# A two-layer graph network on one core: reordering the second probe in the first two blocks of a step, and one activation table for logarithm and exponential

## The chip, the cores and the metric

One core of a Trainium2 chip. The metric is the device time of one execution in microseconds (us), lower is better; "time" is the median of several executions.

## The reference, cut to what matters

Layer 0 is a graph attention layer over 4096 nodes. Layer 1 runs two steps; each makes a 4096 x 4096 attention matrix, keeps of each row the largest probabilities that sum to 0.9, and multiplies the node features by it. This choice of a row's smallest kept value is what the change is about.

```python
def _top_p_attention(X, W1, W2, W3):
    logits = (X @ W1.T @ W2.T) @ (X @ W3.T).T / TAU
    probs = jax.nn.softmax(logits, axis=-1)
    idx = jnp.argsort(-probs, axis=-1)
    sp = jnp.take_along_axis(probs, idx, axis=-1)
    keep_sorted = jnp.cumsum(sp, axis=-1) - sp < TOP_P       # TOP_P = 0.9
    ...                                                      # mask = keep_sorted, back in place
    A = probs * mask
    return A / jnp.maximum(A.sum(-1, keepdims=True), 1e-12)

for n in range(STEPS):                                       # STEPS = 2
    A = _top_p_attention(Xa, W1, W2, W3)
    Xf = R @ Xf
    Xa = A @ Xa
    Z = Z + Xf @ U1[n].T + Xa @ U2[n].T
```

## The kernel before

A step works on 32 blocks of 128 rows. ScalarE (ACT) makes a block's exponentials `e`. Three probes, each a sum over all values below a threshold, close in on the row's cut; the second and third run on VectorE (DVE), and GpSimd (POOL) turns each sum of 128 x 1 values into the next threshold, in some 17 tiny instructions. The third probe leaves the values below its threshold in `big`; DVE takes the largest of these (in step 0, 16 instructions that each give the 8 largest of a stretch, called maxima here, then a sort of the best 48), finds the exact cut and masks `e`. TensorE (PE) turns the masked block and multiplies it.

The tables of a step, one row each for nm (the shift of the exponent) and others, come from a logarithm and an exponential:

```python
nc.vector.tensor_copy(sg, var)
nc.scalar.activation(roots, roots, AF.Ln)                # each of the two needed a table load before it
nc.scalar.activation(roots, roots, AF.Exp, scale=0.5)
nc.vector.scalar_tensor_tensor(nm, sg, 4.0, mu, ALU.mult, ALU.add)
```

The probes and POOL's thresholds (`pool` is GpSimd):

```python
def lowered(c, y, more):
    t = col("lowered", 6)
    pool.tensor_tensor(t, inv_e, y, ALU.pow)                       # "the power" below
    pool.tensor_scalar(t, t, c, more, ALU.mult, ALU.mult)
    return t

def first_step(r):                                                 # after ACT's first probe; cut
    ...
    r.y1 = fall(r, L)
    if not last:
        r.c2 = lowered(r.c1, r.y1, 1.0)                            # threshold of the second probe
        pool.tensor_tensor(r.yy, r.y1, r.y1, ALU.mult)
    pool.tensor_tensor(r.up, r.z, mone, ALU.pow)
    ...

def second_probe(r):
    if r.n + 1 == STEPS:
        return                                                     # the last step has none
    L = col("L")
    nc.vector.scalar_tensor_tensor(junk, r.e, r.c2, r.e, ALU.is_le, ALU.mult, accum_out=L)
    y2 = fall(r, L)
    ...                                                            # 11 more instructions on POOL
    r.c3 = lowered(r.c2, y, up)                                    # threshold of the third probe

def third_probe(r):
    r.L = col("L3")
    nc.vector.scalar_tensor_tensor(big, r.e, r.c3, r.e, ALU.is_le, ALU.mult, accum_out=r.L)

def masked(r):
    kept, r.scale = col("kept"), col("scale")
    nc.vector.scalar_tensor_tensor(r.e, r.e, r.t, r.e, ALU.is_ge, ALU.mult, accum_out=kept)
    nc.vector.reciprocal(r.scale, kept)
```

The order of a block (`candidates` is maxima and sort; `finish` and `finish_rows` are small row work of earlier blocks):

```python
def chosen_kept(b):
    r = blocks[b]
    if 0 < b < NB - 1:
        second_probe(blocks[b + 1])
    candidates(r, found)
    if b == 0:
        masked(r)
    if b > 2:
        finish_scale(blocks[b - 3])
    if b + 2 < NB:
        first_step(blocks[b + 2])
    if b == 0:
        second_probe(blocks[1])
    if b + 1 < NB:
        third_probe(blocks[b + 1])
    if b == 0 and last:
        direct_probe(blocks[3])
    if b > 1:
        finish(blocks[b - 2])
    if b > 2:
        finish_rows(blocks.pop(b - 3))
    if b > 0:
        masked(r)
```

## Time and profile before

| | kernel before |
|---|---|
| time, median of 4 executions | 3262.1 us (3259.44 to 3265.22) |
| the execution that the profile was taken in | 3278.6 us |
| step 0 in the profile | 911.6 us |
| step 1 in the profile | 863.1 us |

"Step 0" is counted from the copy into `roots` ahead of its logarithm to the same copy of step 1, "step 1" from there to the end of the span. First the page's busy times:

```profile
span 3276.4 us, 51761 instructions
PE 2973.4 (91%) x19213; PEld 2417.6 (74%) x19213; DVE 2656.6 (81%) x5020; ACT 1952.7 (60%) x2903; POOL 1266.9 (39%) x1793
```

PE is busiest over the whole span, but the share mixes stages; inside step 0 DVE's chain is the bound, as the prediction shows. Then DVE's groups for the third probe (L694) and the second probe (L673). Columns: busy time and mean ns of one; then the idle time just before them, and what ended it.

```profile
L694 DVE SCALAR_TENSOR_TENSOR big<-e,lowered 128x4096 f32<-128x4096 f32 x64 | 286.8, 4482 | 20.9 <-POOL lowered L639 20.9
L673 DVE SCALAR_TENSOR_TENSOR junk<-e,lowered 128x4096 uint8<-128x4096 f32 x32 | 143.5, 4485 | 14.9 <-POOL lowered L639 14.9
```

The 20.9 hold the 7.27 us that the change aims at. The 14.9 before the second probe are 3.3 for block 0 (a fill of the pipeline) and 11.6 in small pieces.

### The profile page before, as it was taken

The numbers are of one execution on the slowest core, as the hardware profiler recorded it, in microseconds if no ns is written. First come the engines' busy times: TensorE is split into PE (matmuls) and PEld (weight loads), VectorE is DVE, ScalarE is ACT, GpSimd is POOL, SyncE is SP. The second block draws the span as 40 slices with busy tenths as digits, with TensorE's granted clock in tenths as the row PEclk, the third lists the DMA queues.
The fourth block names the chain that finished last, engine by engine and source line by source line (L and its number), as shares of the span: only waits on it lengthen the run. The fifth ranks groups of instructions, "written<-read, shape, count | busy, mean of one in ns | idle before, by whom it ended". The sixth has DMA issues, their size and how long they took to land. (4 is left out here: it accounts for less than half of the span.)

```text
span 3276.4 us, 51761 instructions
## 1 busy us (share of the span) xinstructions
PE 2973.4 (91%) x19213; PEld 2417.6 (74%) x19213; DVE 2656.6 (81%) x5020; ACT 1952.7 (60%) x2903; POOL 1266.9 (39%) x1793
## 2 busy tenths in 40 slices
PE   4499899898989999986899999999879999999996
PEld 2299799797977888874677777777757777777785
DVE  6598899998976555546999999999469988888894
ACT  5588687786862110016577776775266777776742
POOL 3200100201000000003798998899015656656530
PEclk8699999999999999997899999999889999999998
DMA  9825639356225555520000000000100000000000
GB/s 260 228 83 144 204 113 255 117 142 206 73 85 181 165 177 164 161 89 1 10 19 15 16 20 15 15 18 17 62 13 10 25 20 25 22 22 25 20 27 13
DMA packets 198314, 268.48 MB, mean 82 GB/s; under 512 B 13728, under 2 KB 155552, under 8 KB 198048
## 3 DMA queue, kind: packets, MB, share of 16 engines
q1 hardware_dynamic: 152272, 207.99, 19.4%
q0 software_dynamic: 16896, 33.56, 5.7%
q10 hardware_dynamic: 28880, 23.48, 2.3%
q8 instruction: 155, 2.54, 0.3%
q14 instruction: 111, 0.91, 0.1%
HBM read 226.77 MB, written 71.76 MB: 91 GB/s over the span
## 5 line engine op out<-in xcount | busy, mean ns | idle before, releaser
L799 PE MATMUL acc<-X,eT 128*128 128x256 f32 x4160 | 978.4, 381 | 0.8 <-ACT eT L793 0.8
L799 PEld LDWEIGHTS acc<-X,eT 128*128 128x128 f32 x4160 | 762.6, 191 | 90.1 <-ACT eT L793 1.9
L291 PE MATMUL acc<-ut,m 128*128 128x195 bf16 (+1 forms) x8192 | 732.2, 249 | 82.3 <-DVE m L279 49.7
L291 PEld LDWEIGHTS <-m 128*128 128x128 bf16 x8192 | 703.4, 98 | 111.1 <-DVE m L279 66.9
L272 ACT ACTIVATE g<-sr,d_big 128x1024 bf16<-128x1024 f32 x512 | 550.6, 1178 | 50.2 <-DVE m L278 40.6
L618 ACT ACTIVATE void<-e,c 128x2048 int8<-128x2048 f32 x244 | 490.4, 2010 | 0.6
L611 ACT ACTIVATE e<-mm,nm 128x1024 f32<-128x1024 f32 x256 | 285.9, 1117 | 341.2 <-PE mm L488 338.1
L432 PE MATMUL racc<-hl,ar 128*128 128x512 f32 x2048 | 469.4, 391 | 16.8 <-issue 10.0
L432 PEld LDWEIGHTS racc<-hl,ar 128*128 128x128 f32 x2048 | 384.5, 188 | 101.5 <-issue 10.8
L791 PEld LDWEIGHTS tp<-ident,e 128*128 128x128 f32 x2080 | 246.8, 143 | 224.2 <-issue 126.6
L793 ACT COPY eT<-tp 128x512 f32<-128x512 f32 x520 | 303.4, 584 | 168.9 <-PE tp L791 168.1
L791 PE MATMUL tp<-ident,e 128*128 128x128 f32 x2080 | 327.9, 281 | 57.0 <-DVE e L728 42.8
L278 DVE TENSOR_TENSOR m<-g,ax 128x2048 bf16<-128x2048 bf16 x256 | 311.7, 1218 | 41.8 <-ACT g L272 38.8
L707 DVE MAX8 cand<-big 128x8 f32<-128x228 f32 (+1 forms) x1088 | 343.9, 395 | 0.1
L279 DVE TENSOR_TENSOR m<-ax,m 128x2048 bf16<-128x2048 bf16 x256 | 317.1, 1239 | 26.9 <-DVE m L278 1.4
L488 PE MATMUL mm<-kT,qT 64*128 64x512 f32 x1024 | 304.8, 678 | 33.5 <-ACT e L611 33.5
L428 DVE CAST ar<-at 128x1024 fp32r<-128x1024 bf16 x256 | 177.0, 692 | 169.8 <-PE racc L432 167.3
L694 DVE SCALAR_TENSOR_TENSOR big<-e,lowered 128x4096 f32<-128x4096 f32 x64 | 286.8, 4482 | 20.9 <-POOL lowered L639 20.9
L728 DVE SCALAR_TENSOR_TENSOR e<-e,found 128x4096 f32<-128x4096 f32 x64 | 286.7, 4480 | 0.0
L443 ACT ACTIVATE xf<-xf,rinv 128x256 f32<-128x256 f32 x64 | 32.7, 510 | 373.3 <-DVE xf L442 373.3
L648 POOL TENSOR_TENSOR sums<-sums 128x4 f32<-128x4 f32 (+1 forms) x64 | 106.4, 1662 | 378.8 <-ACT void L618 231.1
L488 PEld LDWEIGHTS mm<-kT,qT 64*128 64x128 f32 x1024 | 84.3, 196 | 130.6 <-issue 66.7
(245 smaller groups left out, 3269.4 us busy)
## 6 DMA issues: line engine op xcount, KB each, us to landing
at<-adj_d SPq DMA_DIRECT2D x256, 256.0 KB, 3.0
ut<-uv_d SPq DMA_DIRECT2D x60, 784.0 KB, 4.3
ax<-in_adj_t_dram POOLq DMA_DIRECT2D x32, 1024.0 KB, 13.6
adj_d<-ax SPq DMA_DIRECT2D x32, 1024.0 KB, 11.5
uv_d<-parts ACTq DMA_DIRECT2D x32, 392.0 KB, 8.2
xf<-xf_d SPq DMA_DIRECT2D x65, 128.0 KB, 2.0
sr<-s_d SPq DMA_DIRECT2D x16, 512.0 KB, 4.7
xf_d<-xf ACTq DMA_DIRECT2D x64, 128.0 KB, 2.4
```

Of the source, the lines that this page charges most:

```text
L272: nc.scalar.activation(g[:, c, :], shared[k].sr, AF.Relu, scale=BIG, bias=d_big[:, h, j:j + 1])
L278: nc.vector.tensor_tensor(m[0], g, a, ALU.min)
L279: nc.vector.tensor_tensor(m[1], a, m[0], ALU.subtract)
L291: nc.tensor.matmul(shared[k].acc[i][:, t, :cols], m[t][:, c, ts(i, P)], shared[k].ut[j // QUARTER][:, j % QUARTER, t, :cols], start=(j == ...
L432: nc.tensor.matmul(acc[i].rearrange("p s d -> p (s d)"), ar[:, c, ts(i, P)], hl[hop][:, j].rearrange("p s d -> p (s d)"), start=(j == 0), ...
L488: nc.tensor.matmul(pm[:, h, :], q[ts(h, DA), :], kT[ts(h, DA), ts(c, 512)], start=True, stop=True)
L618: nc.scalar.activation(void, r.e[:, ts(h, N // 2)], (AF.Relu, AF.Sign)[i], bias=r.c1, scale=-1.0, accum_out=r.sums[:, h, 2 + i:3 + i])
L694: nc.vector.scalar_tensor_tensor(big, r.e, r.c3, r.e, ALU.is_le, ALU.mult, accum_out=r.L)
L707: nc.vector.max(cand[:, s, :], big[:, edges[s]:edges[s + 1]])
L791: nc.tensor.transpose(pt[:, i, :], r.e[:, ts(4 * g + i, P)], ident)
L793: nc.scalar.copy(eT, pt)
L799: nc.tensor.matmul(r.acc[:, 0, :], eT[:, i, :], cur[:, j, :], start=(j == 0), stop=(j == NB - 1))
```

## The change

The intent of the reordering: in blocks 0 and 1 DVE should not stand idle while POOL makes the next block's third threshold. So the next block's second probe moves in between this block's maxima and their sort, the sort hides POOL's work, and the mask goes ahead of the next third probe, so that PE gets its block sooner. The intent of the other part: a table that holds both functions, loaded once at the start.

```diff
+    nc.scalar.preload_act_table_set("natural_log_exp_and_others")
...
-    def candidates(r, found):
+    def candidates(r, found, between=None):
...
             nc.vector.max(cand[:, s, :], big[:, edges[s]:edges[s + 1]])
+        if between:
+            between()
         nc.vector.tensor_scalar(cum[:, :1], r.z, 1.0 - TOP_P, r.L, ALU.mult, ALU.subtract)
...
                 r = blocks[b]
-                if 0 < b < NB - 1:
+                early = b < (1 if last else 2)
+                if not early and b < NB - 1:
                     second_probe(blocks[b + 1])
-                candidates(r, found)
-                if b == 0:
+
+                candidates(r, found, (lambda: second_probe(blocks[b + 1])) if early else None)
+                if early:
                     masked(r)
                 if b > 2:
                     finish_scale(blocks[b - 3])
                 if b + 2 < NB:
                     first_step(blocks[b + 2])
-                if b == 0:
-                    second_probe(blocks[1])
                 if b + 1 < NB:
                     third_probe(blocks[b + 1])
...
-                if b > 0:
+                if not early:
                     masked(r)
```

Line numbers in the changed kernel are 3 to 5 higher: third probe L697 (before L694), second probe L676 (L673), mask L733 (L728), POOL's power and threshold L641 and L642 (L638 and L639).

## The prediction

> **What bounds the kernel now.** I read the page first, then each engine's timeline where the changed lines run, then DVE's groups with the idle time before them. The last two of four stages are touched: layer 1 runs two steps, step 0 from about 1453 to 2361 us of the span, step 1 to the end. Each step makes its tables (logarithm, then exponentials), fills the first blocks, and then for each of 32 blocks DVE probes, picks candidates and masks, while PE turns and multiplies the masked block. The start of step 0 on DVE:
>
> ```profile
> 1535.75 5.33 DVE L707 MAX8 cand<-big 128x8 f32<-128x256 f32 x16
> ...
> 1546.36 4.48 DVE L728 SCALAR_TENSOR_TENSOR e<-e,found 128x4096 f32<-128x4096 f32 x1
> ...
> 1550.96 4.49 DVE L673 SCALAR_TENSOR_TENSOR junk<-e,lowered 128x4096 uint8<-128x4096 f32 x1
> ...
> 1562.73 4.49 DVE L694 SCALAR_TENSOR_TENSOR big<-e,lowered 128x4096 f32<-128x4096 f32 x1 [7.27 <-POOL lowered L639]
> ```
>
> These are block 0's maxima (L707), its mask (L728), block 1's second probe (L673) and block 1's third probe (L694). The last waits 7.27 us for POOL, which turns the second probe's sum into the third threshold. Later blocks do not have this wait: there the second probe comes before the maxima, and 10.7 us of maxima and sort hide POOL's 7.1 us. PE's side:
>
> ```profile
> 1550.90 1.12 PE L791 MATMUL tp<-ident,e 128*128 128x128 f32 x4 [5.13 <-DVE e L728]
> ...
> 1591.22 1.09 PE L791 MATMUL tp<-ident,e 128*128 128x128 f32 x4 [13.10 <-DVE e L728]
> ...
> 1813.50 0.63 PE L791 MATMUL tp<-ident,e 128*128 128x128 f32 x4 [0.53 <-DVE e L728]
> ```
>
> PE waits 13.10 us for block 1's mask. From block 2 on it needs 24.32 us a block (one block's first transpose at 1642.48, the next at 1666.80) and DVE needs 24.41, or 25.05 where it waits 0.61 for POOL. DVE's masks of blocks 2 and 30 start at 1610.95 and 2306.92, so 24.86 a block. From 1813 us on, PE waits about 0.5 us in most blocks: **DVE's chain sets the end of step 0**. Step 1 has no second probe (the function returns at once), so PE bounds it after its start.
>
> The table loads, step 0 and then step 1, on ACT:
>
> ```profile
> 1500.63 1.28 ACT L554 ACT_TABLE_LOAD   x1
> 1501.93 0.26 ACT L554 ACTIVATE roots<-roots 128x64 f32<-128x64 f32 x1
> 1502.20 1.28 ACT L555 ACT_TABLE_LOAD   x1
> 1503.50 0.26 ACT L555 ACTIVATE roots<-roots 128x64 f32<-128x64 f32 x1
> ...
> 2413.58 1.28 ACT L554 ACT_TABLE_LOAD   x1 [1.35 <-DVE thr L570]
> 2414.87 0.26 ACT L554 ACTIVATE roots<-roots 128x64 f32<-128x64 f32 x1
> 2415.14 1.28 ACT L555 ACT_TABLE_LOAD   x1
> 2416.44 0.26 ACT L555 ACTIVATE roots<-roots 128x64 f32<-128x64 f32 x1
> ```
>
> One load goes before each logarithm and one before the exponential after it. All work of the step waits for this pair, as DVE's nm needs roots.
>
> The last thing I looked at is the end of step 1. The rare repair ran there, for one block:
>
> ```profile
> 3238.62 4.49 DVE L773 SCALAR_TENSOR_TENSOR e<-junk,a_t,e 128x4096 f32<-128x4096 uint8 x1
> ```
> ```profile
> 3243.26 1.08 PE L791 MATMUL tp<-ident,e 128*128 128x128 f32 x4 [11.85 <-DVE e L773]
> ```
>
> A row whose smallest kept and largest dropped value are equal makes its block be done again. Step 0 had none.
>
> **What the Trainium skill says.** "ScalarE: Activation LUTs", section "What ACT_TABLE_LOAD costs", gives about 1283 ns a load and about 1380 ns of drain. The trace agrees on the load (1283 ns mean); between the end of one small activation and the start of the next it shows 1.31 us (2415.13 to 2416.44), so I use the trace's 1.3. The same page, section "Table sets: the hidden batching unit", says that natural_log_exp_and_others holds both functions and that cheap ones (Relu, Copy) are in every set; so no load should remain in the steps. In its terms, "max 1536 buckets" are shared by a set's functions and each fit has its own error budget, so a logarithm from another set may differ in its last bits. No run shows it yet. "SBUF — State Buffer", section "SBUF: two separate sides", says that a DVE operation with two SBUF inputs and a GpSimd operation exclude one another for a whole instruction. The trace agrees: L649 takes about 0.3 us alone and 4.34 beside the DVE probe at 1510.91.
>
> **The change, part one: tables.** The one load at the start moves from 15.02 us to earlier; ACT then idled until 21.47 us for POOL, so nothing is won. In step 0 the first load lay beside DVE's variance (roots ready at 1501.89), so only the second is won: the exponential can follow the logarithm at about 1502.1 in place of 1503.50, 1.4 us. In step 1 the first load started after its wait, at 2413.58, so both are on the path: 2 x 1.3 = 2.6 us. All that follows in a step waits for it. Sum **-4.0 us**.
>
> **Part two: order in step 0.** Step 1 is unchanged by it: its block 0 already had its mask first, and a second probe does nothing. In step 0 no DVE instruction is added or removed. I laid out the new order by hand with the durations above (a 4096-wide probe 4.41 us to the next start, 16 maxima 5.24, sort 5.37), at old times, without the 1.4:
>
> - Block 0's maxima end 1540.99; second probe of 1 to 1545.40; sort to 1550.77; mask 0 to 1555.2 (before 1550.8, so PE starts **4.4 us later**, 1555.3).
> - POOL's 7.1 us for block 1 start at 1545.58; 5.2 us of them fit beside the sort, then the mask locks POOL out until 1555.2, and 1.7 us are left: third probe of 1 at 1556.9, after a wait of **1.5** and not 7.27.
> - POOL's first step of block 2, which used to run at 1540.5, now stands behind this. Its second instruction is locked out by the third probe until 1561.5; the threshold is ready at 1565.1, in time.
> - Block 1: maxima to 1566.65, second probe of 2 to 1571.1, sort to 1576.4, mask 1 to 1580.8 (before 1591.0, **10 us earlier**), third probe of 2 at 1582.5, again after about 1.5.
> - Block 2 goes back to the old order: second probe of 3 first. Its threshold comes from POOL's first step of block 3, which can begin only at 1582.5, is locked out until 1587.2 and needs 3.6 more: 1590.8. DVE is ready at 1587.0 and **waits about 3.8 us**. So this probe starts at about 1590.9; before it started at 1591.19.
>
> DVE's old 7.27 us thus come back as 1.5 + 1.5 + 3.8 = 6.8. PE multiplies block 0 to about 1582, block 1 at once after it to about 1607, and waits for block 2's mask at about 1615, where it used to be at 1618. The 2.7 us it wins are slack ahead of DVE, which bounds the step from block 10 on anyway. Part two: **-0.3 us**, give or take 2, since 19 or so of the blocks have the 0.61 wait and which do is a matter of tens of ns. With part one: 3261.6 - 4.3 = **3257 us**, if the repair stays as it is.
>
> **The rivals.**
> 1. *The new logarithm reshuffles the ties.* nm comes from logarithm and exponential and is added to every logit before rounding. I recomputed both steps in 32-bit arithmetic from the inputs, over 24 rounding orders and with nm moved by about 1e-6 of its size. Step 0's blocks with a tie did not change by the move. Step 1's were drawn anew: of 48 draws 19 had no such block, 17 one, 9 two, 3 more. What each makes of the time, from this trace: without a repair, block 31's products run as step 0's did (2335.55 to 2358.8, 23.3 us), so from 3203.5 to about 3226.8; four more us of row work end it at about 3231, where now the last DVE instruction ends at 3270.8: -39 us, **3218**. A second block adds a whole preparation and completion one after the other, 6 + 27 + 27 = 60 us: **3318**; a third 3378. Against: the logarithm may be bit-equal, or its change too small. I give 0.8 to a redraw.
> 2. *The reordering pays after all*: POOL gets in more than I allow between DVE's instructions, the wait before block 3's second probe stays under 1 us and DVE keeps 3 us or more. For: POOL's exclusion is read from few instances. It would make 3253 to 3254. PE's own 24.32 us a block caps it at the 2.7 us that PE wins plus little.
> 3. *A worse start*: PE's 4.4 us later first block stays on its path, if block 2's mask is not what it waits for. The hand schedule has 8 us of PE idle time before block 2, so this is unlikely: 3261.
> 4. *Sign is not in the joint set.* L618 alternates Relu and Sign; with two loads for each of its 122 Sign calls ACT would get 122 x 2 x 1.28 = 312 us more, and step 1 is too tight to hide it. The page names cheap functions without Sign in this list, so I keep 0.01.
>
> **Range and chances.** The result has two likely places: about 3257 (repair of one block again, 0.45) and about 3218 (no repair, 0.4); two blocks 0.1, more or other 0.05. Runs of the kernel before lie 6 us apart. The middle of all this is at the upper of the two places: 3257, with 3213 to 3267 to hold both. Faster by 2% would need 3196, below even the case without a repair; slower by 2% is 3327, beyond a second block and reached by a third.
>
> **What would show it.** Right: one table load in all, before 15 us; the idle time before L557 down from 4.9 us in both steps together to about 0.9; before L694 of blocks 1 and 2 waits of 1 to 2 us for POOL, and a new one of 3 to 4 us before L673 of block 3; PE's first block 4.4 us later, its wait before block 1 near zero and a new one of about 8 us before block 2; masks from block 2 on at their old distance. Rival 1: the group of L909 (4 activations for each repaired block) is gone or has 8 or more, or appears in step 0. Rival 2: no wait at block 3's L673 and DVE's masks of blocks 3 on over 3 us earlier than the 1.4. Wrong altogether: more table loads than one, or a step 0 that is longer than before.

## The result, and the profile after

| | before | changed |
|---|---|---|
| time, median of 4 executions | 3262.1 us (3259.44 to 3265.22) | 3259.86 us (3256.99 to 3262.77) |
| ratio | | 0.9993 [0.9976, 1.001] |
| profiled execution | 3278.6 us | 3262.0 us |
| step 0 in the profile | 911.6 us | 896.3 us |
| step 1 in the profile | 863.1 us | 861.0 us |

A ratio is the mean time of one kernel's fast runs over that of the other's fast runs of the same rounds, so it is not quite the ratio of the medians; the brackets are a 95% interval.

So the times agree with the prediction, though this first comparison alone can't tell its -4.3 us from nothing: the interval runs from -7.8 to +3.3 us. And the two profiles seem to tell another story: 15.3 us less in step 0 alone. First the steps that were predicted. The tables, in the timeline of ACT in the changed kernel (start, duration, instruction, idle before):

```profile
1502.80 0.26 ACT L557 ACTIVATE roots<-roots 128x64 f32<-128x64 f32 x1 [1.31 <-DVE roots L556]
1503.09 0.26 ACT L558 ACTIVATE roots<-roots 128x64 f32<-128x64 f32 x1
...
2399.20 0.26 ACT L557 ACTIVATE roots<-roots 128x64 f32<-128x64 f32 x1 [1.37 <-DVE thr L573]
2399.49 0.26 ACT L558 ACTIVATE roots<-roots 128x64 f32<-128x64 f32 x1
```

No load is left in either step; the exponential follows 0.03 us after the logarithm. Among the groups the only load of the program is this one:

```profile
L82 ACT ACT_TABLE_LOAD x1 | 1.3, 1283 | 0.7 <-PEq L1103 0.7
```

Then the order, in the timeline of DVE in the changed kernel, from block 0's third probe on:

```profile
1530.69 4.49 DVE L697 SCALAR_TENSOR_TENSOR big<-e,lowered 128x4096 f32<-128x4096 f32 x1 [7.98 <-POOL lowered L642]
...
1540.45 4.48 DVE L676 SCALAR_TENSOR_TENSOR junk<-e,lowered 128x4096 uint8<-128x4096 f32 x1
...
1550.29 4.48 DVE L733 SCALAR_TENSOR_TENSOR e<-e,found 128x4096 f32<-128x4096 f32 x1
...
1556.34 4.49 DVE L697 SCALAR_TENSOR_TENSOR big<-e,lowered 128x4096 f32<-128x4096 f32 x1 [1.36 <-POOL lowered L642]
...
1581.99 4.49 DVE L697 SCALAR_TENSOR_TENSOR big<-e,lowered 128x4096 f32<-128x4096 f32 x1 [1.36 <-POOL lowered L642]
...
1590.27 4.49 DVE L676 SCALAR_TENSOR_TENSOR junk<-e,lowered 128x4096 uint8<-128x4096 f32 x1 [3.79 <-POOL lowered L642]
```

The wait of 7.27 us is gone, and 1.36, 1.36 and 3.79 us stand in its place, 6.5 in all. PE's first turns of blocks 0, 1 and 2 in the same kernel:

```profile
1554.83 1.12 PE L796 MATMUL tp<-ident,e 128*128 128x128 f32 x4 [10.68 <-DVE e L733]
...
1580.57 0.63 PE L796 MATMUL tp<-ident,e 128*128 128x128 f32 x4 [0.43 <-DVE e L733]
...
1614.70 1.09 PE L796 MATMUL tp<-ident,e 128*128 128x128 f32 x4 [9.61 <-DVE e L733]
```

PE no longer waits before block 1; it waits before block 2 instead. What it won, it lost a block later.

Now the part that was not predicted. DVE's groups after:

```profile
L697 DVE SCALAR_TENSOR_TENSOR big<-e,lowered 128x4096 f32<-128x4096 f32 x64 | 286.8, 4481 | 16.3 <-POOL lowered L642 16.3
L676 DVE SCALAR_TENSOR_TENSOR junk<-e,lowered 128x4096 uint8<-128x4096 f32 x32 | 143.1, 4472 | 7.7 <-POOL lowered L642 7.7
```

The second probe's 7.7 hold 3.3 of block 0 and the new 3.8 of block 3; the 11.6 in small pieces have shrunk to 0.6. DVE's waits between 1560 and 2340 us say it directly. Columns: total, number of times, longest. Before:

```profile
DVE junk L673 <- POOL lowered L639: 11.7, 19, 0.6
```

After (3.8 of the total is block 3's):

```profile
DVE junk L676 <- POOL lowered L642: 4.4, 2, 3.8
```

So of the 15.3 us of step 0, 11 are **18 fewer waits of 0.61 us, in blocks that the change doesn't touch**. About 1.3 is the table (DVE waited 1.80 us for `roots` before its nm, and now 0.53), 0.3 the order. A block without the wait also lasts 24.37 us here in the 24 later blocks, and 24.43 in the kernel before: some 1.4 us more. Of the last 1.3 us, which I didn't follow, 0.7 lie behind block 31's mask.

**What these waits are.** POOL's power makes the threshold for the next second probe. DVE's probes and mask read two inputs from SBUF and shut POOL out while they run (the exclusive lock that the prediction cites; the last section says where the trace departs from it), so POOL's durations show who got in. One block of the kernel before, in its timeline, with a wait:

```profile
1635.36 4.47 DVE L728 SCALAR_TENSOR_TENSOR e<-e,found 128x4096 f32<-128x4096 f32 x1
1635.39 4.86 POOL L638 TENSOR_TENSOR lowered<-inv_e,a 128x1 f32<-128x1 f32 x1
...
1640.36 0.26 POOL L639 TENSOR_SCALAR lowered<-lowered,c 128x1 f32<-128x1 f32 x1
...
1640.65 4.49 DVE L673 SCALAR_TENSOR_TENSOR junk<-e,lowered 128x4096 uint8<-128x4096 f32 x1 [0.62 <-POOL lowered L639]
1640.73 4.82 POOL L659 TENSOR_TENSOR up<-z,mone 128x1 f32<-128x1 f32 x1
```

And the next block of the same execution, without:

```profile
1660.42 4.50 DVE L728 SCALAR_TENSOR_TENSOR e<-e,found 128x4096 f32<-128x4096 f32 x1
1660.46 0.55 POOL L638 TENSOR_TENSOR lowered<-inv_e,a 128x1 f32<-128x1 f32 x1
1661.12 3.94 POOL L639 TENSOR_SCALAR lowered<-lowered,c 128x1 f32<-128x1 f32 x1
...
1665.09 4.49 DVE L673 SCALAR_TENSOR_TENSOR junk<-e,lowered 128x4096 uint8<-128x4096 f32 x1
1665.17 4.82 POOL L659 TENSOR_TENSOR up<-z,mone 128x1 f32<-128x1 f32 x1
```

The power (L638) comes in both 0.03 to 0.04 us after the mask's stamp. In one block it is locked out for the length of the mask (4.86 us), in the other it gets in first (0.55; the mask then takes 4.50 for 4.47). Lost, it makes the second probe wait 0.6 us. The next power, L659, is locked out by the second probe either way (4.82), which keeps POOL late for the next block: I call this the **late phase**. Each of its blocks tosses the coin again; a coin is a way of speaking, for what decides it isn't known. The changed kernel lost once, at 1683, and left the phase in the next block, where the threshold's power came just ahead of the third probe:

```profile
1688.66 4.53 DVE L676 SCALAR_TENSOR_TENSOR junk<-e,lowered 128x4096 uint8<-128x4096 f32 x1 [0.61 <-POOL lowered L642]
1688.73 0.55 POOL L662 TENSOR_TENSOR up<-z,mone 128x1 f32<-128x1 f32 x1
...
1703.71 0.55 POOL L641 TENSOR_TENSOR lowered<-inv_e,a 128x1 f32<-128x1 f32 x1
...
1703.75 4.48 DVE L697 SCALAR_TENSOR_TENSOR big<-e,lowered 128x4096 f32<-128x4096 f32 x1
```

After that POOL stays ahead to the end of the step (the **early phase**): no coin is tossed before the mask any more. What sends an execution there is taken up under "What stays open"; the wait before block 0's third probe, 7.98 us above, turns out to be the sign to watch.

### The profile page after: what moved, and what is told of

Its sections match the earlier page's. It is cut to its first block, busy times and chain, and to the rows that moved or that the text cites. A ratio compares the mean times of both kernels' runs of the same rounds, so it can differ in the third digit from the quotient of the medians.

```text
span 3260.0 us, 51757 instructions
## 1 busy us (share of the span) xinstructions
PE 2970.8 (91%) x19213; PEld 2420.4 (74%) x19213; DVE 2653.5 (81%) x5020; ACT 1944.5 (60%) x2899; POOL 1160.2 (36%) x1793
## 5 line engine op out<-in xcount | busy, mean ns | idle before, releaser
L697 DVE SCALAR_TENSOR_TENSOR big<-e,lowered 128x4096 f32<-128x4096 f32 x64 | 286.8, 4481 | 16.3 <-POOL lowered L642 16.3
L733 DVE SCALAR_TENSOR_TENSOR e<-e,found 128x4096 f32<-128x4096 f32 x64 | 287.1, 4486 | 0.0
```

## The experiments

Theory: the change is worth its table loads and next to nothing of its order, as predicted, and the waits of 0.61 us are a state of an execution, not a work of the change. Rival: the change (its order, or its earlier start by the table) removes the waits and is worth some 15 us, which the timed runs for some reason don't show. Twelve runs of ten kernels were made in three jobs on three chips, each job with its own runs of the kernel before:

| job | runs of the kernel before: median (lowest to highest), number |
|---|---|
| 1 | 3262.6 us (3258.55 to 3280.16), 11 |
| 2 | 3260.32 us (3255.42 to 3271.11), 11 |
| 3 | 3273.64 us (3269.66 to 3276.86), 9 |

What each profile shows of step 0, counted over the second probes of blocks 4 to 31. "Lost" are blocks of the late phase whose coin was lost (each a wait of 0.5 to 0.6 us), "won" those where it was won; "early" are the others, without such a wait. (The early ones of before, b_again, t_only, o_only, nm_big and t_pad are single blocks, after which the late phase went on or began.) The last column is DVE's wait before block 0's third probe. DVE waits there for the same row of POOL's tiny instructions in every kernel, before anything that the edits reorder, so it shows POOL's pace in that execution.

| profile | late, lost | late, won | early | step 0, us | step 1, us | POOL's chain, us |
|---|---|---|---|---|---|---|
| before | 19 | 8 | 1 | 911.6 | 863.1 | 8.02 |
| b_again | 26 | 1 | 1 | 915.0 | 862.6 | 8.02 |
| t_only | 26 | 1 | 1 | 915.2 | 859.7 | 8.02 |
| o_only | 20 | 5 | 3 | 912.0 | 862.6 | 8.02 |
| changed | 1 | 3 | 24 | 896.3 | 861.0 | 7.98 |
| a_again | 1 | 3 | 24 | 896.6 | 861.0 | 7.98 |
| a_again2 | 2 | 14 | 12 | 896.2 | 858.6 | 7.98 |
| nm_shift | 1 | 7 | 20 | 898.0 | 859.5 | 7.99 |
| nm_big | 16 | 5 | 7 | 908.2 | 860.1 | 8.02 |
| no_gap | 7 | 0 | 21 | 898.6 | 860.9 | 7.98 |
| pad_gap | 0 | 0 | 28 | 896.7 | 862.8 | 7.98 |
| t_pad | 0 | 27 | 1 | 896.1 | 858.7 | 8.02 |
| f_first | 0 | 0 | 28 | 894.3 | 858.7 | 7.99 |
| f_first2 | 0 | 0 | 28 | 895.2 | 858.8 | 8.03 |

**b_again: the kernel before, once more** (job 1; no edit).

> The kernel before, unchanged, against itself. My theory: the profiled execution of before (3278.6 us) was an unlucky one: its step 0 had 19 waits of 0.61 us for POOL before second probes (11.6 us together), where the changed kernel's had one, and this is a race of tens of ns between POOL and DVE that the change does not decide. Then timed runs are 3256 to 3266 and ratio 1.000, and a new profile of it has either fewer such waits (under 8) at a time near 3262, or again about 19 at a time near 3275. Rival: the order before always has these waits and the new order removes them; then the profile has about 19 of them again, and its step 0 (first table logarithm of step 0 to that of step 1) is again about 912 us, while timed runs stay at 3262, which would leave the timed gain of only 2 us unexplained.

Measured: 3264.86 us (3259.36 to 3280.41, 7 runs), ratio to the kernel before 1.0003 [0.9989, 1.0016]. Its profile has the waits again, in nearly every block. But the timed runs of the same code lie between 3259.36 and 3280.41, and those of the kernel before likewise between 3258.55 and 3280.16. The waits recur, so they are no accident of the one profile; most timed runs can't have had them all. The profiled execution is one of the timed runs here, and in b_again, t_only and o_only it is the slowest of its list, so taking the profile could favour the waits. That was not tested; but runs of 3275.82, 3278.31 and 3280.16 us in this job left no profile and are as slow, and later profiles have no waits.

**t_only: the table alone** (job 1). Edit to the kernel before:

```diff
+    nc.scalar.preload_act_table_set("natural_log_exp_and_others")
```

> The joint table alone, the order as before. My theory: one table load in all; step 0's tables 1.4 us earlier and step 1's 2.6 us, so 4.0 us less than before, ratio about 0.9988; the repair is drawn anew (step 1 with 0, 1 or 2 blocks, the changed kernel had one, and this kernel's tables are the same, so one again). Rival: the loads lie beside other work, and the saving is under 1 us.

Measured: 3258.54 us (3252.49 to 3274.34), ratio 0.9984 [0.997, 0.9997]. Step 1 lasts 859.7 us against 862.6 and 863.1 with the kernel before. The earlier start by 1.3 us doesn't remove the waits: 26 of them. The gain of the table is there, with its expected size.

**o_only: the order alone** (job 1). Edit to the changed kernel:

```diff
-    nc.scalar.preload_act_table_set("natural_log_exp_and_others")
```

> The new order alone, five table loads as before. My theory: waits of 1.36, 1.36 and 3.79 us for POOL take the place of one of 7.27, so step 0 is 0.5 us shorter and the whole ratio 0.999 to 1.001. Rival (the order frees step 0 from the train of 0.61 us waits): 8 to 11 us shorter, ratio 0.997.

Measured: 3262.12 us (3258.45 to 3277.22), ratio 1.0003 [0.9989, 1.0017]. DVE waits 1.37, 1.37 and 3.81 us in place of 7.27, and 20 of the small waits are in the profile. So the order by itself need not remove them, and it gains nothing measurable. With t_only this refutes the rival's two plain forms.

**a_again, a_again2: the changed kernel, once more** (jobs 1 and 3; no edit).

> The changed kernel again, to narrow its interval. My theory: 4 us below before, ratio 0.9985 to 0.9993, with the three waits of 1.36, 1.36 and 3.79 us in its profile. Whether the train of 0.61 us waits appears in it is open: if it is chance, it may.

> The changed kernel again, as the companion of the other runs of this job. Expected: 3257 to 3261, ratio to before 0.999, step 0 of 896.4 us and one wait of 0.61 us at most three times in its profile.

Measured: 3260.13 us (3254.48 to 3262.56), ratio 0.9994 [0.998, 1.0007]; and 3263.07 us (3256.13 to 3271.51), ratio 0.9979 [0.9966, 0.9993]. The profiles have one and two lost blocks. But in job 3 two runs took 3268.93 and 3271.51 us. Every profiled execution with seven waits or fewer took at most 3262.3 us, and those with 16 or more took 3265.8 to 3280.4, so the changed kernel probably has them too at times. That is inferred from the times; a timed run leaves no trace.

**nm_shift, nm_big: another rounding of the logits** (jobs 2 and 3). Rival 1 of the prediction said that a new logarithm would draw the tied rows anew. These two move the shift nm on purpose, one by about a millionth, one grossly:

```diff
-        nc.vector.scalar_tensor_tensor(nm, sg, 4.0, mu, ALU.mult, ALU.add)
+        nc.vector.scalar_tensor_tensor(nm, sg, 4.0 + 2.0 ** -18, mu, ALU.mult, ALU.add)    # nm_big: 4.25
```

> The changed kernel with the shift of the logits changed by one part in a million of its deviation part (4.0 becomes 4.0 + 2^-18), which leaves the result right but rounds every logit anew. My theory: step 0 needs no repair again, step 1's number of blocks with a tie is drawn anew: none (4 in 10), one (35 in 100), two or more (25 in 100). The repairs are seen from the number of exponentials made again (4 for each block). Without a repair about 39 us shorter (3221), with one the same (3260), with two about 60 longer (3320). Rival: the ties are in the logits themselves and it stays one block.

> The changed kernel with the logits' shift of 4.25 deviations in place of 4, a far larger change than a last bit, result still right. If the tied row is an accident of rounding after the shift, the number of repaired blocks in step 1 should change in about 6 of 10 such draws (0, 1, 2 or more; 39 us less or 60 more for one block less or more). If it stays one block, after three shifts that left it at one (before, the changed kernel, and the shift by one part in a million), the tie is most likely in the logits themselves.

Measured: nm_shift 3258.96 us (2 runs, 3255.94 and 3261.97), ratio 0.9992 [0.9966, 1.0017]; nm_big one run, 3265.81 us, its state unknown. Both still repair one block, in step 1, as did every other kernel here. The exponentials of the repair among the groups of nm_big, 4 for the one block:

```profile
L914 ACT ACTIVATE e<-mm,a_nm 128x1024 f32<-128x1024 f32 x4 | 4.4, 1110 | 3.1 <-POOL x L970 3.0
```

So the redraw to which I gave 0.8 came neither with the new logarithm nor with either of these shifts. The tie probably lies in the logits themselves, before nm is added; that is argued, not shown, and by the prediction's own 17 draws of 48 two shifts would both leave one block by luck in about one case of eight. nm_big shows one more thing: it is the changed kernel but for a constant, and yet it lost 16 coins.

**f_first: POOL's first step earlier** (jobs 2 and 3, the second time as f_first2). In the changed kernel block 3's second probe waits 3.8 us, as POOL makes its threshold late. This runs that work ahead of block 0's and block 1's maxima:

```diff
+                if early and not last:
+                    first_step(blocks[b + 2])
                 candidates(r, found, (lambda: second_probe(blocks[b + 1])) if early else None)
...
-                if b + 2 < NB:
+                if b + 2 < NB and not (early and not last):
                     first_step(blocks[b + 2])
```

> The changed kernel, but in blocks 0 and 1 of step 0 POOL's first step of block b+2 stands ahead of the second probe's work, where POOL is idle for 5.1 us (1539.9 to 1545.0 and 1565.6 to 1570.7 in the changed kernel's trace). My theory: it fits in there, the waits of 1.36 us stay, the wait of 3.79 us before block 3's second probe goes to zero, mask of block 2 comes 3.8 us earlier, PE's wait there falls from 9.6 to about 5.8, and as DVE and PE have the same pace after it (24.36 and 24.33) step 0 is 3 to 4 us shorter: ratio to before 0.997 to 0.9985. Rival: DVE's blocks are held by something else later, and nothing is won; ratio as the changed kernel's, 0.999.

> The kernel with POOL's first steps ahead, again, beside the changed kernel on the same chip. Its profile did not show the gain that I had expected: the wait of 3.79 us went, but one of 1.36 became 5.39, so block 3 starts only 0.2 us earlier. Its 3254.7 us came with 4 to 5 us less before layer 1 than some other runs. My theory: 2 us below the changed kernel (step 0 of 894.3 and not 896.4 us, as it has no 0.61 us wait at all). Rival: 5 us below it, as the first job suggested; or nothing.

Measured: 3254.72 us (3253.48 to 3256.36, 6 runs), ratio 0.998 [0.9965, 0.9995]; and 3255.95 us (3249.49 to 3257.16), ratio 0.9941 [0.9927, 0.9954]. The mechanism that I expected was wrong. The 3.8 are gone, but POOL's earlier work ran into DVE's second probe and was locked out (one instruction took 4.41 us there); DVE's third probe of block 1 waits for it in f_first's timeline:

```profile
1555.25 4.48 DVE L697 SCALAR_TENSOR_TENSOR big<-e,lowered 128x4096 f32<-128x4096 f32 x1 [5.39 <-POOL lowered L642]
...
1580.85 4.49 DVE L697 SCALAR_TENSOR_TENSOR big<-e,lowered 128x4096 f32<-128x4096 f32 x1 [1.37 <-POOL lowered L642]
```

5.39 and 1.37 are 6.76, against 6.51 in the changed kernel. Its advantage is another: in both profiles all blocks are early, in f_first2 at POOL's slower pace too. Its runs were the steadiest in job 2 (2.9 us apart), but not in job 3 (7.7 us, where the kernel before has 7.2).

**no_gap: no gap before the mask** (job 2). If the coin is tossed in the short gap between third probe and mask, where DVE adds a part of an earlier block's result, then moving that work away should lose it always. Edit to the changed kernel:

```diff
-                if b > 1:
+                if b > 1 and last:
                     finish(blocks[b - 2])
-                if b > 2:
+                if b > 2 and last:
                     finish_rows(blocks.pop(b - 3))
                 if not early:
                     masked(r)
+                if b > 1 and not last:
+                    finish(blocks[b - 2])
+                if b > 2 and not last:
+                    finish_rows(blocks.pop(b - 3))
```

> The changed kernel with the short addition of a finished block (0.42 us) moved from between third probe and mask to behind the mask, in step 0 only. My theory of the train of 0.61 us waits: POOL gets one instruction in between third probe and mask if it starts before the mask does, a matter of 30 ns; without the gap it never does, so every block has a wait of 0.3 to 0.6 us for POOL before the second probe and DVE's period is 25.0 us: step 0 is 12 to 17 us longer than the changed kernel's, ratio to before 1.003 to 1.004 in timed runs. Rival: the waits are not from this race, and the period stays at 24.4.

Measured: 3262.03 us (3257.49 to 3263.39), ratio 0.9998 [0.9982, 1.0013]. The expectation was half right. In blocks 3 to 9 every coin was lost, 7 of 7, with waits of 0.51 to 0.55 us; POOL's last instruction before the power was shut out through third probe and mask together (8.7 us). But then, at 1762 us, the kernel fell into the early phase and stayed there. So the gap decides in the late phase, and what I had missed is that there is a second phase in which it doesn't matter.

**pad_gap: a tiny instruction in the gap** (job 2), edit to the kernel before:

```diff
+                if b > 1 and not last:
+                    nc.vector.memset(col("pad"), 0.0)
                 if b > 0:
                     masked(r)
```

> The kernel before with one tiny DVE memset (some 0.07 us) between third probe and mask of step 0's blocks from 2 on. My theory: POOL's instruction now always gets in before the mask, the train of 0.61 us waits is gone from the profile, DVE's period is about 24.45 us where the profiled executions of before had 25.05; profiled time near 3262 and not 3278, timed runs the same as before within 2 us (they mostly run without the train), with fewer of 3268 to 3280 among them. Rival: the profile shows 19 or more such waits again, near 3278.

Measured: 3262.58 us (3257.6 to 3264.95), ratio 1.0001 [0.9986, 1.0017]. No wait at all; but this execution was in the early phase from block 2 on, before the first pad was reached, so for the pad itself it proves nothing. It does show what the order of before is worth without the waits: step 0 lasts 896.7 us, and the changed kernel's, with its table, 896.3. In job 2 the kernel before ran at 3260.32 us, the time of this execution without any wait (3260.8); where few runs have the waits, the pad has nothing to win.

**t_pad: the table and the pad, in the old order** (job 3): the edits of t_only and pad_gap together.

> Old order, joint table, and the tiny memset between third probe and mask: the table without the new order and without the train. My theory: no 0.61 us waits in the profile, step 0 (first logarithm of step 0 to that of step 1) about 895.5 us (896.7 with the pad and five loads), step 1 about 860 us, total near 3258: as the changed kernel or 1 us less. If so the new order is worth nothing. Rival: the order is worth 3 us or more, and this stays at 3261.

Measured: 3255.29 us (3252.96 to 3261.91), ratio 0.9948 [0.9934, 0.9961]. This execution was in the late phase in 27 blocks, and won 27 coins of 27. One of these blocks in its timeline:

```profile
1755.18 4.50 DVE L729 SCALAR_TENSOR_TENSOR e<-e,found 128x4096 f32<-128x4096 f32 x1
1755.21 0.06 DVE L1046 MEMSET pad<- 128x1 f32 x1
1755.21 0.56 POOL L639 TENSOR_TENSOR lowered<-inv_e,a 128x1 f32<-128x1 f32 x1
```

Against 1 won of 27 in t_only, which is the same kernel without the pad and ran at the same pace of POOL (8.02), this is the pad's work, on one execution of each. The stamps are the same as in the lost blocks (the power 0.03 us after the mask); only the durations tell who got in. And t_pad, in the old order, is as fast as f_first2 in the same job and on the same chip (3255.29 and 3255.95 us): with the waits gone, the new order is worth nothing measurable.

Both are faster there than the kernel before (intervals 0.9934 to 0.9961 and 0.9927 to 0.9954), and the changed kernel's interval there (0.9966 to 0.9993) lies above both. That is 0.5 to 0.6% against the kernel before.

## Why the prediction was right, and where not

The time, 3259.86 us against 3257 predicted, lies in the range, and that it would be neither 2% faster nor 2% slower was right. The range of 3213 to 3267 also holds the old time, so it was no hard test. By its steps:

- **Tables, -4.0 predicted.** Right. Step 1 predicted -2.6: the five-load profiles last 862.6 to 863.1 us (mean 862.8), the ten one-load profiles 858.6 to 861.0 (mean 859.7), so -3.1. Step 0 predicted -1.4: DVE's wait for `roots` fell by 1.27. The t_only run, ratio 0.9984, is 5 us, with an interval from 1 to 10. The idle time that the prediction wanted to see shrink to 0.9 in both steps is 1.11: 0.53 and 0.58.
- **The order's waits, 1.5 + 1.5 + 3.8 predicted.** 1.36, 1.36, 3.79 measured. The hand schedule with POOL's lock held to 0.15 us. PE's wait before block 1 near zero: 0.43. The new one before block 2: 9.6 in place of 8.
- **The order's net, -0.3, give or take 2.** Right in the timed runs: o_only has 1.0003. From block 0's second probe to block 3's mask the trace has 116.3 us, with the old order 116.6.
- **Rival 1, a redraw of the ties at 0.8.** Failed. No shift redrew anything. The lower end of the range, 3213, stood on it, and so did the whole second mode at 3218. The recomputation in 32-bit arithmetic on which it stood probably does not describe which rows tie on the chip. (The words "max 1536 buckets" stand on the page that it cites, but in the section "Step-by-step: what each stage is for".)
- **Rival 2, that the order pays after all**, 3253 to 3254: not so. Block 3's wait came. Its cap, the 2.7 us that PE wins "plus little", was wrong by the prediction's own numbers: from PE's block 2 at 1618.15 us, 24.32 us a block lead to 2323.4 for block 31, which came at 2334.65. Without the small waits PE leaves some 11 us more.
- **Rivals 3 and 4** (3261, a worse start; Sign outside the set): PE's later first block was not on the path. One load, and no more.
- **The mis-sized term: the small waits.** The 19 or so blocks with a wait of 0.61 us were read off the profile and carried on as a constant, with 2 us for its change, although 19 x 0.61 are 11.6. It is the largest variable of this kernel: none to 16 us in an execution. I had also not asked why the profile was 17 us slower than the median, which would have led there. The prediction came out right on the time partly by luck: most timed runs in the first comparison evidently had few of these waits before and after. In job 3, where all nine runs of the kernel before lie at 3269.66 us and above, the changed kernel came out 7 us ahead (0.9979).
- **Masks from block 2 on "at their old distance".** Wrong for the profile: 24.37 us in place of 24.43 and 25.05.

**What stays open.** Neither half of the change removes the waits, and the two together mostly do but not always (nm_big). In the profiles of the old order without a pad, 71 lost coins never led out of the late phase. Where the new order left it, POOL's next power had slipped ahead of the second probe, and the threshold's power then came 0.03 to 0.04 us ahead of the third probe. In nm_big and o_only the slip came too, ten times between them, but the threshold's power came some 0.05 us behind the third probe, and the kernel stayed. One of the ten, in nm_big:

```profile
1722.88 4.48 DVE L697 SCALAR_TENSOR_TENSOR big<-e,lowered 128x4096 f32<-128x4096 f32 x1
1722.93 4.85 POOL L641 TENSOR_TENSOR lowered<-inv_e,a 128x1 f32<-128x1 f32 x1
```

The table's last column, which I had overlooked, goes with this. **POOL ran at one of two paces, for a whole execution.** Block 0's third probe waited for the same instructions of POOL, in the kernel before and in pad_gap, which still has its order there:

```profile
1531.22 4.48 DVE L694 SCALAR_TENSOR_TENSOR big<-e,lowered 128x4096 f32<-128x4096 f32 x1 [8.02 <-POOL lowered L639]
1528.18 4.48 DVE L694 SCALAR_TENSOR_TENSOR big<-e,lowered 128x4096 f32<-128x4096 f32 x1 [7.98 <-POOL lowered L639]
```

That is 0.5%, while DVE's probe takes 4.48 us in both. In step 1 the paces part in the same way: the quickest of the 32 chains from POOL's L629 (or its later number) to the power takes 4.03 to 4.04 us in each of the seven slow profiles, and 4.01 to 4.02 in each of the seven quick ones.

From the slipped power to the threshold's, POOL took 14.98 us in the changed kernel (1688.73 to 1703.71) and 15.04 in nm_big (1707.89 to 1722.93), and DVE from its second probe to the third 15.09 and 15.06. Together these are, up to rounding, the step from 0.03 ahead of the third probe to 0.05 behind it. In the old order the same happens at block 3's third probe: 0.05 behind in the four profiles at the slow pace (before, b_again, t_only, t_pad), 0.04 ahead in pad_gap. All five profiles at the slow pace without a pad or f_first's edit have 16 to 26 waits, in both orders; all seven at the quick pace have seven or fewer. So the profile of the kernel before and that of the changed kernel seem to differ mainly by POOL's pace in them. This is read from 14 executions, not set by an experiment.

It remains open what sets the pace, why in the new order at the slow pace some lost coins lead to a slip (11 of 36, one of these in the last block) and in the old none, and whether the change makes the quick pace likelier: its three profiles have the quick one and the two of the kernel before the slow one, and job 3's 7 us would fit that, but nm_big (slow) and pad_gap (quick) show that it doesn't decide it. Nor can the waits of a timed run be seen.

## What to carry to other kernels

When two profiles differ by much more than the timed runs do, look for many equal small waits before crediting the change, and run the unchanged kernel again with a profile: it may be in another phase. Then compare the time of an untouched chain on each engine between the two profiles: here 8.02 against 7.98 us told the executions apart. A chain of small GpSimd instructions beside long DVE instructions with two inputs was a row of coin tosses here; a tiny instruction in the right gap (t_pad) and an earlier start of the chain (f_first2) settled them, each in one profile at the slow pace. And moving a wait helps only if the engine that is waited for gets time to work in: here each reordering returned the 7.27 us as 6.5 to 6.8 elsewhere.

## What the Trainium skill lacked or had wrong

- "SBUF — State Buffer", section "SBUF: two separate sides", says that whichever operation starts first gets the port pair for the whole instruction. The durations agree for DVE's part: POOL's power takes 0.55 us where it gets in and 4.86 where the mask shuts it out. They do not agree for POOL's part: with the power's 0.55 us inside it, the mask takes 4.50 us in place of 4.47 or 4.48, so it isn't held up for POOL's whole instruction. The page lacks two things. Start stamps in a trace don't show who was first: the power is stamped 0.03 to 0.04 us after the mask both where it got in and where it was shut out. And such a lock can settle into a phase that repeats in every block: 26 waits of 0.61 us in one execution (b_again), none in another (pad_gap), 915.0 and 896.7 us for the same step; the waits are 15.9 of these 18.3 us.
- "ScalarE: Activation LUTs", section "What ACT_TABLE_LOAD costs", counts 1380 ns of drain besides the load of 1283 ns. Between two small activations the trace of the kernel before has room only for the load: 1.31 us from the end of one to the start of the next. Nor does the page's list of what is in every set name Sign, while one load serves all of this kernel's logarithms, exponentials, Relu and Sign calls, with a correct result.
- None of the pages says that a profiled execution can be in another mode than the timed ones: 3278.6 us against 3259 to 3265. Nor that GpSimd's pace differs by execution: the same chain took 8.02 to 8.03 us in seven profiles and 7.98 to 7.99 in the other seven.
